# A 3x3 filter of one of three channel blocks on TensorE as 32x32 diagonal tiles, in place of VectorE

## The chip, the cores and the metric

One core of a Trainium2 chip runs the whole program. The metric is device microseconds of one execution, lower is better. TensorE (PE; PEld for its weight loads), VectorE (DVE), ScalarE (ACT) and GpSimd (POOL) work side by side, each in the order of its own queue; the queue of SyncE (SP) issues the transfers. Matrix products land in PSUM banks, from which VectorE or ScalarE copy them out ("evacuate") to SBUF.

## The reference, cut to what matters

32 images of 56 x 56 tokens and 96 channels, fp32, pass through four layers. The change is in layer 0.

```python
# layer 0: x is [32, 56, 56, 96]; E = 4 experts, M = 384 hidden channels
rw = sigmoid(mean(x, (1, 2)) @ Wr + br)                  # router: [32, 4]
h = einsum('bhwc,bcm->bhwm', x, einsum('be,ecm->bcm', rw, Wpw)) + rw @ bpw
h = relu(bn1(h))                                         # 384 channels
h = sum_e rw[:, e] * (conv3x3_depthwise(h, Wdw[e]) + bdw[e])   # <- the filter in question
h = relu(bn2(h))
h = einsum('bhwm,bmf->bhwf', h, einsum('be,emf->bmf', rw, Wpwl)) + rw @ bpwl
x = bn3(h) + x
# layer 1: x + a fixed 5x5 depthwise filter
# layer 2: relu, 3x3 depthwise filter, 96x96 pointwise product, batch norm
# layer 3: windows of 7x7 of the image shifted by 3: layer norm, attention of 3 heads with
#          a mask, projection, residual; layer norm, gelu perceptron 96-384-96, residual
```

A depthwise filter treats each channel by itself. Since the experts are mixed linearly, one mixed kernel of nine taps per channel and image is enough.

## The kernel before, in words

Channels lie on partitions for layers 0 to 2, tokens for layer 3. The 384 hidden channels are three blocks of 128 (`NB`). The image is worked in two halves of 28 rows for layer 0, in 8-row strips for layer 1 (`conv5`, L368) and in rows of windows, 7 image rows or 392 tokens, for layers 2 and 3.

`stage_conditional` is layer 0 of one image. It loads and transposes the image (L216, L231, L232), finds the router weights (L242 to L251; one small product on L246), and mixes the experts: `wmix` and `wmix2`, the weights of the two pointwise products, and `mix`, per channel the nine taps and two biases. `biasd` and `s2` are the bias and scale of the second batch norm. Then, for each half and block k:

- `expand` multiplies by `wmix` in four pieces (L293) and ScalarE evacuates them with batch norm and relu into `h1` (L300), a block with a border of zeros that GpSimd sets (L286 to L289). There are two `h1` buffers, and a block is expanded ahead of the filter of the block before it.
- The filter is nine VectorE instructions over 128 x 1568 elements: L324 multiplies the first tap's view by its tap, L326 multiplies the next view and adds.
- ScalarE applies batch norm and relu to the block (L329).

When the three blocks of a half stand in `h2` (one buffer), four products per half sum over the blocks (L344), ScalarE evacuates them (L352), and GpSimd adds the image into `x1` (L353), which layer 1 reads.

`stage_depthwise` is layers 1 and 2: 25 diagonal 96x96 products a strip on TensorE (L368, evacuated on L377), a 3x3 filter of 96 channels on VectorE (L390, L392), a GpSimd copy of the border (L393), and a product (L402, L409). `stage_swin` is layer 3: `normalized` and `transposed` for the norms (L448 to L466, with L83 and L84 for the reciprocal root), projections (L478 to L490), scores per head (L502 to L515, on 32 rows of TensorE), weighted sums per head (L527 to L535, on 32 columns of it), L543, and the perceptron (L559, L560, L566, L574, stores on L581 to L588).

Three images are under way, each in another stage. The stages are Python generators, and `interleave` draws their steps side by side, each at an even pace by its number of steps (91, 44 and 42), which sets the order on every engine:

```python
stages.append((stage_conditional(step), 42))
interleave(stages)
```

All products but those of the attention share the four PSUM banks of the pool `mm`; `att` has three and one more for `po`. A strip of layer 1 holds its bank from its first to its 25th product, across many steps of the others.

Of the kernel before, what the change touches and what calls it, by code (L numbers as in the profile page):

```python
# [11 lines left out]
F32 = mybir.dt.float32  # L12
AF = mybir.ActivationFunctionType
# [5 lines left out]
C = 96  # L19
M = 384  # L20
E = 4
P = 128
NB = 3  # blocks of 128 among the 384 hidden channels
NROW = 8  # rows of windows, 7 image rows each
RT = 7 * W  # tokens of a row of windows
PK = 98  # tokens of a pack: two neighbouring windows, a block of 7 x 14 tokens
NP = 4  # packs in a row of windows
NH = 3
# [5 lines left out]

# columns of the 384-channel vectors
V_BPW, V_BDW, V_G1, V_B1, V_M1, V_V1, V_G2, V_B2, V_M2, V_V2, V_MLP, V_WDW = 0, 4, 8, 9, 10, 11, 12, 13, 14, 15, 16, 17
NV = V_WDW + 36
# columns of the 96-channel vectors
U_BPWL, U_G3, U_B3, U_M3, U_V3, U_DWB, U_LN1G, U_LN1B, U_LN2G, U_LN2B, U_DWK = 0, 4, 5, 6, 7, 8, 9, 10, 11, 12, 13
# [3 lines left out]
def attention_mask():  # L43
    """Additive mask of a pack's 98 x 98 scores: [ordinary or last row of windows, query, pack, key]."""
    m = np.zeros((2, PK, NP, PK), np.float32)
    r, c = np.divmod(np.arange(PK), 14)
    for last in range(2):
        for j in range(NP):
            col = 14 * j + c
            group = col // 7 * 10  # L50
            group = group + np.where(col >= 53, 1, 0)
            if last:
                group = group + np.where(r >= 4, 5, 0)
            m[last, :, j, :] = np.where(group[:, None] == group[None, :], 0.0, NEG)
    return m
# [3 lines left out]
def kernel(ctx: ExitStack, tc: tile.TileContext, a: dict, mask: bass.AP, out: bass.AP):  # L59
# [11 lines left out]

# [1 line left out]
    ident = const.tile([P, P], F32, name="ident")  # L73
# [6 lines left out]
    def rsqrt(dst, src, eps, scale=1.0):  # L80
        """dst = 1 / sqrt(src * scale + eps), for few elements."""
        n = src.shape[0]
        nc.vector.tensor_scalar(dst, src, scale, eps, ALU.mult, ALU.add)  # L83
        nc.gpsimd.tensor_tensor(dst, dst, mhalf[:n, : dst.shape[1]], ALU.pow)  # L84
# [50 lines left out]

    # batch norms of layer 0 as scale * y + shift
    def bn(g, b, m, v, n, name):
# [11 lines left out]

    # what the router mixes per channel: nine taps and two biases, experts innermost  # L150
    NM = 11
# [6 lines left out]

    # layer 1: its kernel's taps on diagonals, the residual in the centre's
    k5 = load([C, 25], a["L1_conv_kernel"].rearrange("c a b -> c (a b)"), "k5")  # L160
# [4 lines left out]

    # layer 2: pointwise weights scaled by its batch norm, and the biases in one row
    pw = load([C, C], a["L2_conv_pw_kernel"].rearrange("a b c f -> (a b c) f"), "pw")
# [19 lines left out]

    # layer 3
    wq = load([C, C], a["L3_conv_wq"], "wq")
# [8 lines left out]

    # images with zero borders
    x1 = big.tile([C, H + 4, W + 4], F32, name="x1")  # L200
# [3 lines left out]

    # rows of x1 that layer 1 of the image before no longer reads
    consumed = [H]

    def stage_conditional(b):
        """Layer 0 of image b, into x1."""
        xT = two.tile([C, H * W], F32, tag="xT", name="xT")  # L210
# [28 lines left out]

        # router, the same on all partitions  # L240
        pooled = small.tile([C, 1], F32, tag="pooled", name="pooled")
# [10 lines left out]

        # mixtures of the experts
        wmix = work.tile([C, M], F32, tag="wmix", name="wmix", bufs=1)
# [18 lines left out]
        nc.vector.tensor_tensor(biasd, mix[:, :, 10], s2, ALU.mult)  # L273
        nc.vector.tensor_tensor(biasd, biasd, t2, ALU.add)
        prod3 = small.tile([C, E], F32, tag="prod3", name="prod3", bufs=2)
        nc.vector.tensor_tensor(prod3, c96[:, U_BPWL : U_BPWL + E], rw[:C], ALU.mult)
# [5 lines left out]
        def expand(half, k):  # L282
            # rows first .. first + 28 of the image at rows at .. of h1; the row beyond the image is zero
            first, at = (0, 1) if half == 0 else (HALF - 1, 0)
            h1 = two.tile([P, HALF + 2, W + 2], F32, tag="h1", name="h1")
            nc.gpsimd.memset(h1[:, :, 0:1], 0.0)  # L286
            nc.gpsimd.memset(h1[:, :, W + 1 : W + 2], 0.0)
            edge = 0 if half == 0 else HALF + 1
            nc.gpsimd.memset(h1[:, edge, :], 0.0)  # L289
            r = 0  # L290
            for n in (8, 7, 7, 7):
                pt = mm.tile([P, 512], F32, tag="mm", name="pt")
                nc.tensor.matmul(  # L293
                    pt[:, : n * W],
                    wmix[:, k * P : (k + 1) * P],
                    xT[:, (first + r) * W : (first + r + n) * W],
                    start=True,
                    stop=True,
                )
                nc.scalar.activation(  # L300
                    h1[:, at + r : at + r + n, 1 : W + 1],
                    pt[:, : n * W].rearrange("p (r w) -> p r w", w=W),
                    AF.Relu,
                    bias=bias1[:, k : k + 1],
                    scale=s1[:, k : k + 1],
                )
                r += n
            return h1

        # a block's expansion is traced ahead of the filter of the block before  # L310
        blocks = [(half, k) for half in range(2) for k in range(NB)]
        h1 = expand(*blocks[0])
        yield
        for at, (half, k) in enumerate(blocks):
# [3 lines left out]
            acc = h2[:, k].rearrange("p (r w) -> p r w", w=W)  # L318
            for t in range(9):
                dy, dx = divmod(t, 3)  # L320
                tap = mix[:, k, t : t + 1]
                view = h1[:, dy : dy + HALF, dx : dx + W]
                if t == 0:
                    nc.vector.tensor_scalar(acc, view, tap, None, ALU.mult)  # L324
                else:
                    nc.vector.scalar_tensor_tensor(acc, view, tap, acc, ALU.mult, ALU.add)  # L326
                if t % 3 == 2:
                    yield
            nc.scalar.activation(  # L329
                h2[:, k], h2[:, k], AF.Relu, bias=biasd[:, k : k + 1], scale=s2[:, k : k + 1]  # L330
            )
            h1 = h1_next
# [4 lines left out]
            for n in range(4):  # L337
                r = half * HALF + 7 * n
                # the image before has to have left these rows of x1
                while consumed[0] < r + 7:  # L340
                    yield
                pt = mm.tile([P, 512], F32, tag="mm", name="pt")
                for q in range(NB):
                    nc.tensor.matmul(  # L344
                        pt[:C, :RT],
                        wmix2[:, q * C : (q + 1) * C],
                        h2[:, q, n * RT : (n + 1) * RT],
# [13 lines left out]
    def stage_depthwise(b, res):  # L361
        """Layers 1 and 2, from x1 to res: tokens of the shifted image on partitions."""
        def conv5(i):
# [51 lines left out]

        # a row's matrix product is traced well behind its filter
        packed = []
        done = 0
        for i in range(7):
            for n, _ in enumerate(conv5(i)):  # L420
                yield
                if n == 1 and packed:
                    pointwise()
                    # rows up to 8 i - 2 have both neighbours
                    if 7 * done + 10 < 8 * i:
# [19 lines left out]
    def normalized(src):  # L445
        """src, [98, 4, 96] with tokens on partitions, less its mean and by its deviation."""
        mu = small.tile([PK, NP], F32, tag="mu", name="mu")
# [12 lines left out]
    def transposed(d, g, bta):  # L460
        """The layer norm of a normalized d, with channels on partitions."""
        pt = mm.tile([P, 512], F32, tag="mm", name="pt")
# [6 lines left out]
    def stage_swin(b, res):  # L469
        """Layer 3 on the shifted image in res, packs of two windows on partitions."""  # L470
        def project(i):
# [78 lines left out]
        def perceptron(i):  # L550
# [25 lines left out]
            )  # L576
            # back to the unshifted image; the last rows and columns wrap around
            for j in range(NP):
# [11 lines left out]

        # a row's weighted sums are traced behind the scores of the next row
        rows_of, probs, normed = {}, {}, {}
# [24 lines left out]
    def interleave(stages):  # L617
        """Traces the stages' steps side by side, each at an even pace by its number of steps."""
        todo = [[0, n, g] for g, n in stages]
# [5 lines left out]

    # three images at a time, each in another part of the chain
    residuals = {}
    for step in range(B + 2):
# [7 lines left out]
        if step < B:  # L636
            stages.append((stage_conditional(step), 42))
        interleave(stages)


def build(nc, shapes, batch):
    """The program on nc for inputs of these shapes."""
    a = {k: nc.dram_tensor(f"in_{k}", s, F32, kind="ExternalInput").ap() for k, s in shapes.items()}
# [17 lines left out]
```

## Time and profile before

| | |
|---|---|
| median of 2 runs | 10090.53 us (10088.93 to 10092.14) |
| span of the profiled execution | 10095.2 us |
| mean granted TensorE clock | 0.974 |
| TensorE busy | 9488.0 us, 94%, 47622 matmuls |
| VectorE busy | 7154.6 us, 71% |
| ScalarE busy | 4210.8 us, 42% |
| GpSimd busy | 3729.8 us, 37% |
| DMA | mean 9 GB/s |

The first row is from unprofiled runs; everything below it is one profiled execution. Busy time is the union of an engine's instructions, and matmuls are pipelined: the recorded length of one contains time in which the next already streams, so the spacing of their starts says more than their length. "idle before, releaser" tells how long an engine stood still before a group's instructions and what ended most of that.

In the profile, the program is a ramp of two periods (first only layer 0, then layers 0 to 2), 30 alike with all three stages, and a tail in which the last images leave.

### The profile page before, as it was taken

To read this page: it belongs to the slowest core of one execution; us is meant where nothing else is said; L and a number is where in the kernel's file an instruction comes from. 1 tells how busy PE (TensorE), PEld (TensorE's weight loads), DVE (VectorE), ACT (ScalarE), POOL (GpSimd) and SP (SyncE) were. 2 spreads that over 40 slices of the span, in tenths; PEclk is the share of its full clock that TensorE was granted. 3 is DMA by queue.
4 is the path that set the end of the run, shared out by engine and by line. 5 is a ranking of instruction groups with operands and counts; after the bars stand their busy time and mean duration, and the time that the engine had idled before them with its cause. 6 is when DMAs were issued, how large, how long until landed. Compare 5 with 4: busy or idle time off the path is not lost.

```text
span 10095.2 us, 132019 instructions
## 1 busy us (share of the span) xinstructions
PE 9488.0 (94%) x47622; PEld 5516.7 (55%) x47622; DVE 7154.6 (71%) x11221; ACT 4210.8 (42%) x11520; POOL 3729.8 (37%) x3406
## 2 busy tenths in 40 slices
PE   5999999999999999999999999999999999999998
PEld 2455555555555555555555555555555555555556
DVE  6767767678777677676787776776767877767743
ACT  2344444444444444444444444444444444444434
POOL 2234334334333343333433333433434433334323
PEclk8999999999999999999999999999999999999996
DMA  0000000000000000000000000000000000000000
GB/s 21 5 10 7 6 9 11 10 9 6 7 10 10 10 7 6 9 10 10 9 6 7 10 10 10 7 6 9 10 10 9 6 7 10 10 10 7 4 5 9
DMA packets 164927, 88.06 MB, mean 9 GB/s; under 512 B 138455, under 2 KB 164272, under 8 KB 164272
## 3 DMA queue, kind: packets, MB, share of 16 engines
q1 hardware_dynamic: 164272, 79.62, 3.0%
q8 instruction: 375, 6.14, 0.2%
q14 instruction: 280, 2.29, 0.1%
HBM read 40.95 MB, written 38.54 MB: 8 GB/s over the span
## 4 chain that ended last, share of the span: by engine, by line
PE 77%; DVE 10%; POOL 6%; ACT 3%; issue 2%; SPq 1%; DMA 0%; POOLq 0%; DVEq 0%; ACTq 0%
PE pt L368 37%; PE po L535 6%; PE pt L566 5%; PE ps L502 5%; PE pt L344 4%; PE pt L293 4%; DVE d L392 4%; PE pt L559 3%; DVE h L326 3%; POOL lnd L457 2%; PE ps L527 2%; PE pt L478 2%; PE pt L543 2%; POOL var L84 2%; PE pt L482 2%
## 5 line engine op out<-in xcount | busy, mean ns | idle before, releaser
L368 PE MATMUL pt<-x,diag 96*96 96x448 f32 x11200 | 4643.9, 549 | 9.9 <-ACT h L300 9.9
L326 DVE SCALAR_TENSOR_TENSOR h<-h,mix,h 128x1568 f32<-128x1568 f32 x1536 | 2887.5, 1888 | 4.3
L368 PEld LDWEIGHTS pt<-x,diag 96*96 96x96 f32 x11200 | 1683.3, 163 | 1765.3 <-issue 1670.8
L515 POOL TENSOR_TENSOR s<-s,den 98x392 f32<-98x392 f32 x768 | 822.5, 1071 | 2480.1 <-DVE den L514 2469.5
L392 DVE SCALAR_TENSOR_TENSOR d<-x,c,d 96x392 f32<-96x392 f32 (+2 forms) x2304 | 1470.0, 649 | 11.2 <-ACT x L377 7.6
L511 ACT ACTIVATE s<-s,top 98x98 f32<-98x98 f32 x3072 | 1114.6, 366 | 475.7 <-DVE top L508 475.1
L84 POOL TENSOR_TENSOR var<-var,mhalf 98x4 f32<-98x4 f32 x512 | 714.3, 1395 | 784.3 <-DVE var L83 536.2
L504 DVE TENSOR_TENSOR s<-ps,masks 98x392 f32<-98x392 f32 x768 | 429.0, 559 | 647.4 <-PE ps L502 646.7
L552 POOL TENSOR_TENSOR tb<-res,L_conv_b 98x384 f32<-98x384 f32 x256 | 506.3, 1978 | 1029.9 <-DVE res L546 567.8
L566 PE MATMUL pt<-w,hid 128*98 128x96 f32 x6144 | 693.1, 266 | 171.4 <-ACT hid L560 159.4
L566 PEld LDWEIGHTS pt<-w,hid 128*98 128x98 f32 x6144 | 657.5, 179 | 322.6 <-ACT hid L560 242.6
L535 PEld LDWEIGHTS po<-pT,v 98*32 98x32 f32 x6144 | 508.2, 111 | 508.0 <-ACT pT L532 334.0
L502 PEld LDWEIGHTS ps<-kT,qT 32*98 32x98 f32 x6144 | 589.0, 164 | 324.6 <-issue 248.5
L492 POOL TENSOR_TENSOR xb<-res,L_conv_bo 98x384 f32<-98x384 f32 x256 | 451.1, 1762 | 836.4 <-DVE res L546 592.2
L457 POOL TENSOR_TENSOR lnd<-lnd,var 98x384 f32<-98x384 f32 x512 | 724.9, 1416 | 40.2
L535 PE MATMUL po<-pT,v 98*32 98x98 f32 x6144 | 678.3, 254 | 64.5 <-ACT pT L532 49.1
L502 PE MATMUL ps<-kT,qT 32*98 32x98 f32 x6144 | 713.9, 258 | 3.3 <-ACT qT L479 3.3
L300 ACT ACTIVATE h<-pt,bias,s 128x392 f32<-128x392 f32 (+1 forms) x768 | 497.6, 687 | 381.9 <-PE pt L293 342.3
L559 PE MATMUL pt<-hT,w 96*128 96x392 f32 x1536 | 562.0, 502 | 86.3 <-ACT hT L466 86.2
L466 ACT ACTIVATE hT<-pt,c 96x392 f32<-96x392 f32 x512 | 342.7, 669 | 705.2 <-PE pt L464 705.1
L344 PE MATMUL pt<-h,wmix 128*96 128x392 f32 x1536 | 568.8, 501 | 61.2 <-ACT h L329 37.7
L293 PE MATMUL pt<-xT,wmix 96*128 96x392 f32 (+1 forms) x1536 | 583.8, 514 | 28.6 <-ACT h L300 24.5
(112 smaller groups left out, 10735.7 us busy)
## 6 DMA issues: line engine op xcount, KB each, us to landing
xin<-in_x SPq DMA_DIRECT2D x256, 147.0 KB
out<-o SPq DMA_DIRECT2D x1792, 4.1 KB
out<-o SPq DMA_DIRECT2D x1792, 1.1 KB
out<-o SPq DMA_DIRECT2D x672, 36.8 KB
out<-o SPq DMA_DIRECT2D x96, 21.0 KB
out<-o SPq DMA_DIRECT2D x96, 15.8 KB
wpw<-in_L_conv_Wpw SPq DMA_DIRECT2D x1, 576.0 KB
wpwl<-in_L_conv_Wpwl SPq DMA_DIRECT2D x4, 144.0 KB
```

The source lines that it names most:

```text
L84: nc.gpsimd.tensor_tensor(dst, dst, mhalf[:n, : dst.shape[1]], ALU.pow)
L293: nc.tensor.matmul(pt[:, : n * W], wmix[:, k * P : (k + 1) * P], xT[:, (first + r) * W : (first + r + n) * W], start=True, stop=True,)
L326: nc.vector.scalar_tensor_tensor(acc, view, tap, acc, ALU.mult, ALU.add)
L344: nc.tensor.matmul(pt[:C, :RT], wmix2[:, q * C : (q + 1) * C], h2[:, q, n * RT : (n + 1) * RT], start=(q == 0), stop=(q == NB - 1),)
L368: nc.tensor.matmul(o, diag5[:, t], x1[:, 8 * i + dy : 8 * i + dy + 8, dx : dx + W], start=(t == 0), stop=(t == 24),)
L392: nc.vector.scalar_tensor_tensor(acc, view, tap, acc, ALU.mult, ALU.add)
L457: nc.gpsimd.tensor_tensor(d, d, var[:, :, None].to_broadcast([PK, NP, C]), ALU.mult)
L502: nc.tensor.matmul(ps[:PK, js], qT[hs, js], kT[hs, js], start=True, stop=True)
L511: nc.scalar.activation(s[:, j], s[:, j], AF.Exp, bias=top[:, j : j + 1], accum_out=den[:, j : j + 1])
L535: nc.tensor.matmul(po[hs, js], v[:, j, hs], pT[:, js], start=True, stop=True)
L559: nc.tensor.matmul(pt[:, :RT], w1[:, k * P : (k + 1) * P], hT, start=True, stop=True)
L566: nc.tensor.matmul(pt[:PK, j * C : (j + 1) * C], hidden[k][:, j * PK : (j + 1) * PK], w2[:, k], start=(k == 0), stop=(k == NB - 1),)
```

## The change

The third block of each half (k = 2) is filtered on TensorE. A tap of a block is a diagonal 128x128 matrix; only its four 32x32 diagonal tiles are not zero, and these are multiplied by themselves, each on its own 32 rows and 32 columns of the array. Two row chunks of 392 tokens are done at a time, in two banks: the first writes tile g to output partitions of group g, the second ("turned") to those of the next group, so that the eight products of a tap use eight different tiles of the array. The turned chunk thus comes out with its channels rotated by 32 partitions, and the bias, the scale and the weights of the next product are kept in a rotated copy as well (`biasdt`, `s2t`, `wmix2t`), made by two small transfers each in the SyncE queue. `taps` holds the nine diagonals of an image.

```diff
+    eye32 = const.tile([P, 32], F32, name="eye32")
+    nc.vector.tensor_tensor(eye32, ident[:, 0:32], ident[:, 32:64], ALU.add)
+    nc.vector.tensor_tensor(eye32, eye32, ident[:, 64:96], ALU.add)
+    nc.vector.tensor_tensor(eye32, eye32, ident[:, 96:128], ALU.add)
+
+    def turn(dst, src):
+        nc.sync.dma_start(out=dst[32:], in_=src[:96])
+        nc.sync.dma_start(out=dst[:32], in_=src[96:])
+
+    s2t = const.tile([P, 1], F32, name="s2t")
+    turn(s2t, s2[:, NB - 1 :])
...
+        wmix2t = work.tile([P, C], F32, tag="wmix2t", name="wmix2t", bufs=1)
+        turn(wmix2t, wmix2[:, (NB - 1) * C :])
+        biasdt = small.tile([P, 1], F32, tag="biasdt", name="biasdt", bufs=2)
+        turn(biasdt, biasd[:, NB - 1 :])
+        taps = work.tile([P, 9, 32], F32, tag="taps", name="taps")
+        nc.vector.tensor_tensor(
+            taps,
+            eye32[:, None, :].to_broadcast([P, 9, 32]),
+            mix[:, NB - 1, 0:9, None].to_broadcast([P, 9, 32]),
+            ALU.mult,
+        )
...
-            for t in range(9):
+            if k == NB - 1:
+                for pair in range(2):
+                    banks = [mm.tile([P, 512], F32, tag="mm", name="pt") for _ in range(2)]
+                    for t in range(9):
+                        dy, dx = divmod(t, 3)
+                        for turned in range(2):
+                            r = 7 * (2 * pair + turned) + dy
+                            for g in range(4):
+                                to = 32 * ((g + turned) % 4)
+                                nc.tensor.matmul(
+                                    banks[turned][to : to + 32, :RT].rearrange("c (r w) -> c r w", w=W),
+                                    taps[32 * g : 32 * g + 32, t],
+                                    h1[32 * g : 32 * g + 32, r : r + 7, dx : dx + W],
+                                    start=(t == 0),
+                                    stop=(t == 8),
+                                )
+                    for turned in range(2):
+                        at = (2 * pair + turned) * RT
+                        nc.scalar.activation(
+                            h2[:, k, at : at + RT],
+                            banks[turned][:, :RT],
+                            AF.Relu,
+                            bias=biasdt if turned else biasd[:, k : k + 1],
+                            scale=s2t if turned else s2[:, k : k + 1],
+                        )
+                    yield
+            for t in range(9) if k < NB - 1 else ():
...
-            nc.scalar.activation(
-                h2[:, k], h2[:, k], AF.Relu, bias=biasd[:, k : k + 1], scale=s2[:, k : k + 1]
-            )
+            if k < NB - 1:
+                nc.scalar.activation(
+                    h2[:, k], h2[:, k], AF.Relu, bias=biasd[:, k : k + 1], scale=s2[:, k : k + 1]
+                )
...
-                        wmix2[:, q * C : (q + 1) * C],
+                        wmix2t if n % 2 and q == NB - 1 else wmix2[:, q * C : (q + 1) * C],
...
-            stages.append((stage_conditional(step), 42))
+            stages.append((stage_conditional(step), 40))
```

## The prediction

> **What bounds the kernel now.** I read the page first: engines, chain, costliest groups.
>
> ```profile
> PE 9488.0 (94%) x47622; PEld 5516.7 (55%) x47622; DVE 7154.6 (71%) x11221; ACT 4210.8 (42%) x11520; POOL 3729.8 (37%) x3406
> PE 77%; DVE 10%; POOL 6%; ACT 3%; issue 2%; SPq 1%; DMA 0%; POOLq 0%; DVEq 0%; ACTq 0%
> L368 PE MATMUL pt<-x,diag 96*96 96x448 f32 x11200 | 4643.9, 549 | 9.9 <-ACT h L300 9.9
> L326 DVE SCALAR_TENSOR_TENSOR h<-h,mix,h 128x1568 f32<-128x1568 f32 x1536 | 2887.5, 1888 | 4.3
> ```
>
> TensorE is busy 94% of the span and carries 77% of the chain that ended last; VectorE, where the filter sits (L326), has 29% of the span free. Counts matter too: L368 is called 32 x 7 x 25 = 5600 times and appears 11200 times, so an fp32 matmul is two passes here, each with a weight load.
>
> Next the windows view over the 28 periods from 746 to 9380 us, in which three images are under way (a period, from one router matmul on L246 to the next, is 308.3 us), and the waits of TensorE in the same stretch:
>
> ```profile
> 746.00:9380.00 8634.00, 8230.00 (x41662) 4777.92 (x41662) 6259.54 (x9772) 3678.55 (x10080) 3274.12 (x2968) 0.99 0.03 9
> PE pt L566 <- ACT hid L560: 147.9, 57, 4.0
> PE pt L464 <- POOL lnd L457: 91.5, 56, 1.7
> PE pt L559 <- ACT hT L466: 77.4, 84, 1.1
> PE po L535 <- ACT pT L532: 46.5, 85, 1.9
> PE pt L478 <- ACT h L300: 15.1, 28, 0.6
> PE po L535 <- DVE pT L530: 11.2, 29, 0.4
> PE pt L566 <- DVE res L409: 11.0, 28, 0.4
> ```
>
> The columns are length, then busy time of PE, weight loads, DVE, ACT and POOL, then the granted clock. TensorE idles (8634 - 8230) / 28 = 14.4 us a period, at clock 0.99, and nearly all of it is ended by ScalarE or GpSimd, not by the filter. VectorE is busy 224 of 308 us. Work taken off VectorE can therefore give back a part of 14.4 us a period; work put on TensorE is paid almost in full.
>
> Last, the timeline, for what passes cost and whether small ones overlap (start, length, count at the end):
>
> ```profile
> 5013.13 0.82 PE L482 MATMUL pt<-hT,wk 96*96 96x392 f32 x2
> 5011.53 0.93 PE L502 MATMUL ps<-kT,qT 32*98 32x98 f32 x8
> 5005.64 1.36 PE L502 MATMUL ps<-kT,qT 32*98 32x98 f32 x16
> 5036.32 0.86 PE L535 MATMUL po<-pT,v 98*32 98x98 f32 x8 [0.20 <-ACT pT L532]
> 9806.91 1.24 PE L535 MATMUL po<-pT,v 98*32 98x98 f32 x16
> ```
>
> Of two 392-column passes (L482) the second adds 0.33 us; start to start of such passes is 329 ns at the median (L344, L293, L559 alike). L502 uses 32 rows of the array per head, L535 32 columns per head. Eight passes of one head follow at 84 to 87 ns. Sixteen of two heads would need 1.6 us in a row, and take 1.36 and 1.24: in the single starts, the second head's first pass begins 4 to 5 ns after the first head's fifth, and then both go on at 82 to 89 ns each. So passes on different rows, and passes on different columns, do run side by side at full pace, two at a time. More than two is not shown.
>
> **The change, part by part.** *Removed*, a third of the block filter: from VectorE 2887.5 / 3 + 219.6 / 3 (L324) = 1036 us, 32 us a period; from ScalarE a third of L329, 108 us. *Added to ScalarE*: 256 evacuations of 128x392, at L300's 676 ns = 173 us. Net +65 us, 2 us a period, on an engine 42% busy: hidden; were it the bound, +65 us. *Added to VectorE*: the 128x288 product `taps`, nearest the 128x288 step of L259 at 0.51 us, 16 us in all, hidden in the 84 us that VectorE has free a period. *Added to SyncE*: four small copies an image for `wmix2t` and `biasdt` (behind them in the queue stand stores of finished rows, which come only in the last third of a swin stage), and two for `s2t`, ahead of the loads of the later constants and of the first image. There the queue waits for s2, written at 14.96 us where SyncE stood at 13.66; two issues at about 0.4 us: +2 us at the start, once.
>
> *Added to TensorE*, which decides: 32 images x 2 halves x 2 pairs x 9 taps x 2 x 4 = 9216 calls, 18432 passes of 392 columns. L502 and L535, the small ones of before, are two passes as well. One after the other they cost 329 ns: 6064 us. The eight tiles of a tap differ in rows, columns or both. Ends for a pass: 41 ns with eight at once (758 us), 165 ns with the two at once that the trace shows (3032 us). I take 46 ns: in the L535 pair the second head's first pass starts 370 ns after the first head's, so TensorE took in eight passes with their weight loads in that time, and no row shows it faster: 848 us. The two kinds of pair shown are the two relations that neighbours among the eight have, and no pair slowed its partner.
>
> [...] Here four row tiles write one bank, on different partitions; the L502 pair wrote two banks, so no run here shows it. [...]
>
> Ends of a burst: 128 bursts of 144 passes. Changing between L368 and the column-tiled L535 costs 91 ns more than staying (466 against 375 ns into it, 175 against 84 out of it); twice that and 0.16 us until the eight are under way are 0.35 us: 44 us. TensorE gains 892 us of work, 27.9 us in each of 32 periods.
>
> *Waits.* In the period of 5064 to 5373 us one stretch of the chain runs through the block filter, while the layer-2 filter and a GpSimd copy stand behind it:
>
> ```profile
> 5102.88 1.80 DVE h L326
> 5108.78 0.96 DVE d L392
> 5109.73 1.76 DVE h L326
> 5112.10 2.31 POOL d L393
> ```
>
> It costs TensorE 0.71 + 1.38 us around it. With a third of the filter gone, and the bursts giving ScalarE and GpSimd time to catch up, I take 4 us a period back; bounds 0 and 14.4. Against it, each burst needs two of the four `mm` banks while a layer-1 sum holds one and the next block's expansion fills the rest, so up to three L300 evacuations (2 us) may stand before it, with every later matmul behind it: 0 to 8 us a period, taken as 3. The stage's pace, 40 steps in place of 42, moves work by less than one step: nothing.
>
> *The ramp.* In the first period TensorE is idle anyway, but the next half's filter waits for `h2` and so for L344. A half's third block took 8 x 1.86 + 1.03 us of VectorE and 1.70 of ScalarE; two bursts take 13.9 us and an evacuation: -3 us a half, -6. In the second period TensorE streams only some 150 of 238 us: nothing, with -10 and +28 as bounds.
>
> Sum: 30 x (27.9 - 4 + 3) = 807, -6, +2: +803 us on the profiled 10095.2 us, 10898. The median of the runs, 10090.5, lies 4.7 us below that span: **10893 us**, 8% slower. Its own range: 10406 (41 ns, all idle time recovered, no new waits) to 11163 (46 ns, nothing recovered, 8 us of new waits).
>
> **Rivals.** *Four at once.* Tiles on the same rows take turns, 82 ns a pass: 1511 + 44 us, 48.6 a period; 30 x 47.6 + 16 in the first period + 2 = +1446: 11536 us. For it: the L502 pair is on different rows. Against: the L535 pair shares all its rows and overlapped.
> *Two at once*, or banks that exclude one another: 3032 + 44, 96.1 a period, +2884 and some 110 in the first two periods: 13085 us. For it: no row has more than two. Against: in neither pair did the second stream slow the first. *One at a time* gives 190.9 a period and about 16100 us; both pairs speak against it.
> *Not slower.* The place is VectorE's in-order queue: if the filter's 1.9 us instructions are what holds up the softmax and norm chains that TensorE waits for, their removal pays for the bursts. Beyond plain streaming, the starts of matmuls show 39.5 us a period, idle time, mode changes and short waits together. To end within 2% (202 us, 6.7 a period) 21.2 of these must vanish at 46 ns, 18.4 at 41 ns; at 25 recovered the time is about 10175. For it: L326 is the next largest group after L368. Against: idle time is 14.4 of the 39.5, ended by ScalarE and GpSimd.
>
> **How the numbers follow.** Eight tiles mostly side by side 0.64, four at once 0.16, two at once 0.07, one at a time 0.03, not slower 0.07, the rest between these. Range 10600 to 11600: the first case but for its lower tail, and the second. About 2% is what a measurement of this kernel can tell from no change. Faster by over 2% needs 34.6 of the 39.5 us to vanish: 0.02; within 2%: 0.05; slower: 0.93.
>
> **What would show it.** Right: about 66000 matmul records; the new line at 18432 passes, bursts of 6 to 7 us, a period near 335 us; VectorE's busy time down by about 1020 us; TensorE busy 95% or more. Bursts of 12 us mean four at once, of 24 two. Wrong altogether: a period at or below 308 us, or new waits ahead of the bursts above 8 us a period.

## The result and the profile after

The changed kernel takes 10602.98 us (10600.68 to 10605.28), the kernel before 10090.53 us: a ratio of 1.050, 95% interval 1.048 to 1.052. It is slower, as forecast, by 512 us where 802 were forecast, at the lowest end of the range. The profiled execution spans 10598.9 us at a granted clock of 0.983.

From the page of the changed kernel, engines, chain and the groups that answer to those of before (layer 1 is now L420, the block filter on VectorE L377, the new passes L353):

```profile
PE 10242.0 (97%) x66054; PEld 5897.7 (56%) x66054; DVE 6153.5 (58%) x10680; ACT 4283.1 (40%) x11712; POOL 3451.2 (33%) x3406
PE 86%; DVE 9%; ACT 2%; issue 1%; POOL 1%; SPq 0%; DMA 0%; DVEq 0%; ACTq 0%; POOLq 0%
L420 PE MATMUL pt<-x,diag 96*96 96x448 f32 x11200 | 4582.1, 545 | 0.0
L377 DVE SCALAR_TENSOR_TENSOR h<-h,mix,h 128x1568 f32<-128x1568 f32 x1024 | 1916.0, 1878 | 3.5
L353 PE MATMUL pt<-h,taps 32*32 32x392 f32 x18432 | 850.2, 504 | 97.2 <-ACT h L362 74.2
```

VectorE is 1001 us lighter, and L353 has 18432 passes. Their 504 ns are the length of one, which overlaps others: together they keep TensorE busy for 850 us, 46 ns each with the ends of the bursts and passes at half clock among them. TensorE carries 86% of the chain in place of 77%; GpSimd has nearly left it, 1% after 6%.

The timeline shows the four bursts of one period, the fourth in two rows (start, length, count):

```profile
5064.14 6.31 PE L353 MATMUL pt<-h,taps 32*32 32x392 f32 x144
5075.08 6.16 PE L353 MATMUL pt<-h,taps 32*32 32x392 f32 x144
5193.95 6.16 PE L353 MATMUL pt<-h,taps 32*32 32x392 f32 x144
5200.51 0.86 PE L353 MATMUL pt<-h,taps 32*32 32x392 f32 x8
5203.84 7.83 PE L353 MATMUL pt<-h,taps 32*32 32x392 f32 x136 [2.47 <-ACT h L362]
```

A burst without a wait takes 5.67 to 5.82 us from its first to its last start, some 40 ns a pass (40.4 below). The single starts show passes mostly 6 to 8 ns apart, all eight in a row or, in the first burst of a period, four and, 180 ns behind the first of them, the four of the other chunk; each tile follows again after 329 ns: eight streams at full pace. The fourth burst follows 0.4 us behind the third; after eight passes it waits for the third's banks, which ScalarE is still to evacuate (L362). That makes it 8.98 us long; in 17 of 28 periods it takes 10.67 us, because after the wait TensorE also runs 3.4 us at half clock.

The windows view over 27 periods, 1084 to 9868 us (length, busy time of PE, weight loads, DVE, ACT and POOL, then the clock), and TensorE's waits in them:

```profile
1084.00:9868.00 8784.00, 8576.66 (x55734) 4928.44 (x55732) 5188.19 (x8966) 3610.19 (x9882) 2934.81 (x2862) 0.99 0.03 9
```

```profile
PE pt L618 <- ACT hid L612: 70.6, 28, 2.6
PE pt L353 <- ACT h L362: 66.8, 27, 2.5
PE pt L611 <- ACT hT L518: 59.7, 81, 1.1
PE po L587 <- ACT pT L584: 5.6, 27, 0.2
```

TensorE idles (8784 - 8577) / 27 = 7.7 us a period, 14.4 before. The wait for the norm on GpSimd (`lnd`, 91.5 us before) is gone, that for `pT` nearly so, that for `hid` halved; the one for the banks is new.

One accounting serves all runs below. From the starts of TensorE's passes, each gap is compared with the spacing of such passes back to back (375 ns for 448 columns, 329 for 392, 83 for 98); over 100 ns beyond it counts as a wait, 40 to 100 as a mode change ("changes and less" adds what is under 40), and time from start to start inside bursts is counted apart. In us a period:

| | period | streaming | changes and less | waits | bursts |
|---|---|---|---|---|---|
| before | 308.4 | 269.5 | 19.5 | 19.4 | |
| after | 325.4 | 270.8 | 19.8 | 7.6 | 27.2 |

So the bursts cost 27.2 + 1.3 (their last passes) + 0.3, and 11.8 of waits went away: +17.0 a period, 510 us in 30 periods.

A wait of this accounting is not only standing still: TensorE is idle in 14.4 of the 19.4 us and in 5.2 of the 7.6, and recorded busy in the rest, with the end of the pass ahead or with a slower pass. In the same periods the clock stood at half for 8.2 us a period before and 4.6 after; 1.7 of the 5.0 us of recorded work and 0.1 of the 2.4 lie in gaps that touch such a stretch.

### The profile page after: what moved, and what is told of

It reads as the page before. It is cut to its first block, busy times and chain, and to the rows that moved or that the text cites. A ratio compares the mean times of both kernels' runs of the same rounds, so it can differ in the third digit from the quotient of the medians.

```text
span 10598.9 us, 168961 instructions
## 1 busy us (share of the span) xinstructions
PE 10242.0 (97%) x66054; PEld 5897.7 (56%) x66054; DVE 6153.5 (58%) x10680; ACT 4283.1 (40%) x11712; POOL 3451.2 (33%) x3406
## 4 chain that ended last, share of the span: by engine, by line
PE 86%; DVE 9%; ACT 2%; issue 1%; POOL 1%; SPq 0%; DMA 0%; DVEq 0%; ACTq 0%; POOLq 0%
PE pt L420 37%; PE ps L554 6%; PE pt L353 6%; PE po L587 6%; PE pt L396 5%; PE pt L618 5%; PE pt L318 4%; DVE h L377 4%; DVE d L444 4%; PE pt L611 4%; PE ps L579 2%; PE pt L530 2%; PE pt L539 2%; PE pt L595 2%; PE pt L534 2%; PE pt L454 2%
## 5 line engine op out<-in xcount | busy, mean ns | idle before, releaser
L420 PE MATMUL pt<-x,diag 96*96 96x448 f32 x11200 | 4582.1, 545 | 0.0
L420 PEld LDWEIGHTS pt<-x,diag 96*96 96x96 f32 x11200 | 1678.6, 162 | 1760.0 <-issue 1683.9
L377 DVE SCALAR_TENSOR_TENSOR h<-h,mix,h 128x1568 f32<-128x1568 f32 x1024 | 1916.0, 1878 | 3.5
L444 DVE SCALAR_TENSOR_TENSOR d<-x,c,d 96x392 f32<-96x392 f32 (+2 forms) x2304 | 1408.1, 630 | 294.8 <-ACT x L429 277.1
L84 POOL TENSOR_TENSOR var<-var,mhalf 98x4 f32<-98x4 f32 x512 | 674.9, 1318 | 1124.1 <-DVE var L83 1094.3
L353 PE MATMUL pt<-h,taps 32*32 32x392 f32 x18432 | 850.2, 504 | 97.2 <-ACT h L362 74.2
L604 POOL TENSOR_TENSOR tb<-res,L_conv_b 98x384 f32<-98x384 f32 x256 | 469.2, 1833 | 1058.7 <-DVE res L598 800.3
L618 PE MATMUL pt<-w,hid 128*98 128x96 f32 x6144 | 667.4, 260 | 81.2 <-ACT hid L612 79.4
L353 PEld LDWEIGHTS pt<-h,taps 32*32 32x32 f32 x18432 | 401.6, 107 | 503.6 <-issue 357.3
L544 POOL TENSOR_TENSOR xb<-res,L_conv_bo 98x384 f32<-98x384 f32 x256 | 330.1, 1289 | 993.6 <-DVE res L598 784.6
L509 POOL TENSOR_TENSOR lnd<-lnd,var 98x384 f32<-98x384 f32 x512 | 618.7, 1208 | 40.1
```

The source lines that it names most:

```text
L353: nc.tensor.matmul(banks[turned][to : to + 32, :RT].rearrange("c (r w) -> c r w", w=W), taps[32 * g : 32 * g + 32, t], h1[32 * g : 32 * g ...
L420: nc.tensor.matmul(o, diag5[:, t], x1[:, 8 * i + dy : 8 * i + dy + 8, dx : dx + W], start=(t == 0), stop=(t == 24),)
L509: nc.gpsimd.tensor_tensor(d, d, var[:, :, None].to_broadcast([PK, NP, C]), ALU.mult)
L618: nc.tensor.matmul(pt[:PK, j * C : (j + 1) * C], hidden[k][:, j * PK : (j + 1) * PK], w2[:, k], start=(k == 0), stop=(k == NB - 1),)
```

## The experiments

Unless an interval is given, a run is one execution with a profile, beside a run of the kernel before (10087 to 10111 us). Theory A: the waits left because VectorE's queue got shorter. Theory B: because the others catch up during a burst. Theory D, formed on the way: because the three stages meet in another order.

**Load VectorE again.**

```diff
+                    spare = big.tile([P, 24, W], mybir.dt.bfloat16, tag="spare", name="spare")
+                    for t in range(5) if pair == 0 else range(4, 9):
...
+                        nc.vector.scalar_tensor_tensor(spare, view, tap, centre, ALU.mult, ALU.add)
                     yield
```

> The changed kernel, with VectorE loaded again: beside the bursts it does ten instructions over 24 rows of the third block (into a spare tile that nothing reads), about the work that was taken off it. Theory A (relief): the 11.8 us a period by which TensorE's waits shrank, 19.4 to 7.6, came from VectorE's shorter queue; loaded again, they return, 30 x 11.8 = 354 us: about 10955. Theory B (cover): the waits shrank because other engines catch up while TensorE works through a burst; then the load costs little: 10600 to 10650.

10931.5 us: 328 us more, as A says (the load comes in lumps of five instructions, where the filter's came in threes). Only 3.9 us a period are returned as plain waits (11.5); 6.0 stand inside the bursts (33.2), where the banks come free later. From 784 to 9800 us of this run, where the changed kernel had 66.8 in its stretch:

```profile
PE pt L353 <- ACT h L362: 155.3, 27, 5.9
```

**Relief without bursts.** The third block is not filtered at all; L329 reads `h1`.

> The kernel before without the third block's filter on any engine: ScalarE's batch norm and relu read the expanded block instead, so the output is not the reference's; all else and the pace of 42 steps stay. Theory A (relief): 11.8 us a period fall away, and 2 x 16 us in the first period: about 10090 - 354 - 40 = 9700. Theory B (cover): only the ramp gains: about 10050.

9973.9 us: 114 us below the run of before beside it, far from A's 390; some 36 of them fall in the first two periods. The waits fall from 19.4 to 15.1, that is 4.2 us a period, and 1.4 return as mode changes. So the relief by itself is worth what the prediction took, and A does not explain 11.8; nor does the result of the first run fit B. Each theory failed once.

**Same tiles for both chunks.**

```diff
-                                to = 32 * ((g + turned) % 4)
+                                to = 32 * g
```

> The changed kernel with both chunks of a pair on the same four diagonal tiles (second chunk not turned; rotated copies are made but not used). If the two chunks overlap only because they use different tiles, a pass costs 82 ns in place of 41, a burst 11.8 us in place of 5.9, 23.6 us a period: about 10603 + 700 = 11300, less what the longer bursts cover (up to 7 us a period, 11090). If what sets the pace of a burst is how fast TensorE takes in instructions, nothing changes: about 10600.

11227.6 us. From this run's timeline:

```profile
5177.35 12.06 PE L353 MATMUL pt<-h,taps 32*32 32x392 f32 x144
```

81 ns a pass from start to start: chunks on the same tile took turns, chunks on neighbouring tiles of the same rows did not (40.4 ns in the changed kernel). Turning the second chunk is worth 19 us a period. The waits stay at 7.7: bursts of twice the length cover no more of them.

**Every burst twice.**

```diff
-                    for t in range(9):
+                    for t in [*range(9), *range(9)]:
```

> The changed kernel with every burst's nine taps done twice (the second time starts the sums anew, so the output is the same). It adds 576 passes of 40.4 ns, 23.3 us a period. If TensorE now bounds the period with nothing left to win, it is paid in full: 30 x 23.3 + 20 in the ramp = +720, about 11320. Theory B (cover) lets the longer bursts cover more of the 7.6 us of waits that are left: +17 a period, about 11110.

11263.0 us, bursts 46.9 us a period, waits 7.8. The second nine taps cost 23.3 less the 3.9 us of the bank wait, which is gone, now that there is time to evacuate. TensorE's added work is paid in full, and B falls in the form that longer bursts cover more.

**One step between the bursts of a half.**

```diff
                     yield
+                    if pair == 0:
+                        yield
-            stages.append((stage_conditional(step), 40))
+            stages.append((stage_conditional(step), 42))
```

> The changed kernel with one more step of the other stages between the two bursts of a half (42 steps in place of 40). In the changed kernel the fourth burst of a period stands 0.4 us behind the third, starts eight passes and waits for the third's banks to be evacuated: bursts take 27.2 us a period where four of 5.8 would take 23.3. If that wait comes from the two bursts standing together, it goes: 30 x 3.9 = -117, about 10485. If the evacuations are late whatever stands between (ScalarE's queue), or the shift brings other waits, the time stays at 10600.

11017.0 us. The bank wait is gone as meant (bursts 23.2), but the waits elsewhere rise from 7.6 to 23.5 us a period; the clock stands at half for 23.3 us a period (4.6 in the changed kernel), and in 10.5 of the 23.5 TensorE is recorded busy. One step more in one stage undid more than all that the change had won: from here comes theory D.

**Bursts of one tap.** The filter of the third block is left out but for its centre.

> The changed kernel with bursts of one tap (the centre) in place of nine, so that the filter of the third block is left out but for its centre and the output is not the reference's. TensorE has 20.7 us less to do a period. The relief of VectorE alone left 15.1 us of waits (run e2), the changed kernel has 7.6, and bursts of double length 7.8. Theory B2 (cover by the length of the bursts): with hardly any burst the waits go back to about 15: period 325.4 - 3.9 - 20.7 + 7.5 = 308, total about 10080. Theory D (order): the waits left because the work of the stages meets in another order, so they stay at 7.6 to 8: period 301, total about 9860.

9915.0 us. With bursts of 2.1 us a period in all, the waits are 10.2, nearer D's 8 than B's 15.

**One number.** `interleave` draws a step from the stage that is furthest behind its number of steps. Changing that number for layer 0 adds and removes no instruction.

```diff
-            stages.append((stage_conditional(step), 42))
+            stages.append((stage_conditional(step), 40))
```

> The changed kernel with one number back as it was: layer 0 is paced as if it had 42 steps, and still has 40. No instruction is added or removed. Theory A/B (relief of VectorE and cover by the bursts made the waits of TensorE shrink from 19.4 to 7.6 us a period): 10600, within 50. Theory D (the pace sets the order in which the three stages meet, and with it the waits; one step more, run e5, already brought 23.5 us of waits): the waits change by several us a period, the time by 100 us or more, most likely up, to 10700 to 11000.

> The kernel before with the pace number of the changed one: layer 0 paced as if it had 40 steps. Nothing else changes. Theory A/B: as before, 10090 within 50. Theory D: the waits move between 8 and 24 us a period, the time by 100 us or more either way; if 40 is the lucky number in itself, 11 us a period fall away: about 9750.

> The kernel before with layer 0 paced as if it had 44 steps. As for 40: no change by theory A/B, 100 us or more either way by theory D. The two runs together give the spread that the order alone makes in a kernel without any bursts.

> The kernel before, layer 0 paced as if it had 41 steps. Theory D alone (the order sets the waits, bursts or not): among a few pace numbers some give waits as low as the changed kernel's 7.6 us a period, a time down to 9750. Theory D2 (the low waits need the bursts too, which give the other engines time): without bursts the waits stay at 15 us or more at any pace, 9950 or more.

> The kernel before, paced as if layer 0 had 43 steps. As for 41: theory D a time anywhere from 9750 to 10480; theory D2 9950 or more.

> The changed kernel, paced as if layer 0 had 38 steps. Theory D: waits anywhere from 7 to 25 us a period as in the kernel before, 10550 to 11050. Theory D2: waits below those of the kernel before at most paces, 7 to 17 us, 10550 to 10800.

> The changed kernel, paced as if layer 0 had 44 steps: as for 38.

> The kernel before at pace 46. Of five paces (40 to 44) the waits of TensorE were 29.6, 24.1, 19.4, 11.5 and 19.0 us a period. If a faster pace of layer 0 is better in itself, they are below 15 here: under 9970. If the order is a lottery, anything from 9850 to 10480, about 10130 the mean of the five.

| pace number | before: us, waits a period | after: us, waits a period, bursts |
|---|---|---|
| 38 | | 10621.9, 11.1, 23.4 |
| 40 | 10478.5, 29.6 | **10603.0**, 7.6, 27.2 |
| 41 | 10269.6, 24.1 | |
| 42 | **10090.5**, 19.4 | 10774.5, 17.1, 22.8 |
| 43 | 9855.6, 11.5 | |
| 44 | 10161.8, 19.0 | 10531.7, 9.3, 22.9 |
| 46 | 10604.6, 34.5 | |

The pace alone moves the kernel before between 9856 and 10605 us, more than the change did, and the changed kernel by 243. The granted clock is the lower the longer the time: 0.942, 0.956, 0.974, 0.978, 0.957 and 0.935 at 40, 41, 42, 43, 44 and 46 of the kernel before, and at 46 TensorE is recorded busy in half of the 34.5 us (17.8). Whether it is the waits that bring the clock down was not tried. At 40, with TensorE's waits from 1084 to 9368 us, it is the norm chain that the kernel before waits for most:

```profile
PE pt L464 <- POOL lnd L457: 184.1, 52, 4.3
PE pt L293 <- ACT hid L560: 85.0, 52, 2.2
PE pt L402 <- ACT dp L395: 81.6, 26, 3.1
```

Theory D holds, but not alone, and not within its stated bounds: pace 44 moved the kernel before by 53 us, where 100 or more were expected, 40 brought 29.6 us of waits, where 24 were the most named, 46 a time above its 10480, and the changed kernel at 44 ended just below its 10550. D2, without bursts 9950 or more at any pace, falls with 43. The mean of the waits is 23.0 us over six paces of the kernel before and 11.3 over four of the changed one, in which they are lower at each of the three numbers that both ran. At a like number the change costs 125, 684 and 370 us (40, 42, 44). Paired instead by the distance from its own count of steps (before 40, 42, 44, 46 with after 38, 40, 42, 44), it costs 143, 512 and 613 us and gains 73; best against best, 9856 and 10532, it costs 676. The 11.8 us do not split into two fixed parts either: by way of the changed kernel at 42 the change takes 2.3 and the number 9.5; by way of the kernel before at 40 the number adds 10.2 and the change takes 22.0. So part of the 11.8 us goes with the change (4.2 by relief alone), and the rest depends on the order; how much is cover by the bursts is not settled by so few paces.

**The kernel before at pace 43, timed.**

> The kernel before with layer 0 paced as if it had 43 steps, once more and timed: 9855 us, 2.4% below the kernel before, within 0.3%. If the first look was a chance of one run and not of the order, it falls back towards 10100.

9844.0 us (9828.5 to 9857.9), ratio to the kernel before 0.974, interval 0.972 to 0.977. It beats both, by a number. TensorE's waits from 738 to 9300 us:

```profile
PE pt L559 <- ACT hT L466: 95.0, 57, 2.8
PE pt L566 <- ACT hid L560: 54.9, 57, 2.8
PE pt L464 <- POOL lnd L457: 12.4, 29, 0.5
```

The same instructions run, 47622 passes on TensorE; the wait for `lnd` shrinks from 91.5 to 12.4 us.

**Tiles where TensorE already works.** If tiles overlap so well, layer 1, 96 channels of diagonals, should gain.

```diff
+            halves = [mm.tile([P, 512], F32, tag="mm", name="pt") for _ in range(2)]
...
+                            halves[n][32 * (g + n) : 32 * (g + n) + 32, : 4 * W].rearrange("c (r w) -> c r w", w=W),
+                            diag5[gs, t, gs],
+                            x1[gs, r : r + 4, dx : dx + W],
```

> The kernel before, its block filter on VectorE as it was, with layer 1 (L368, the costliest group) on 32x32 diagonal tiles: a strip of 8 rows is two halves of 4 rows, the second half one column group to the right in a bank of its own, so that six passes of 224 columns run side by side; the second half comes out 32 partitions further and is evacuated in three pieces. If six overlap as the eight did, a strip takes 50 x 187 ns = 9.4 us in place of 19, 68 us a period less on TensorE: period about 255 (VectorE's 224 us busy come near), total about 8550. If taking in passes at 31 ns is too fast and 41 ns is the limit: 86 us in place of 65 for layer 1, total about 9100. If the rows' tiles exclude each other here: no gain, 10100 or more.

> v1 with the tiles only in strips 1, 3 and 5 of layer 1; the other four strips keep the 96x96 form. In v1 the granted clock was 0.83: the trace has stretches of 82 us at half clock in which TensorE stood still for under 2 us and ran layer 1's tiles and the small products of the attention. If full-array work is what brings the clock back, it is over 0.95 here, TensorE has 28 us a period less to do, and with some more waits the period is about 290: 9550. If the clock stays at 0.83 with these few tiles too, nothing is won: 10300 or more.

> The changed kernel with layer 1 on tiles as in v1. If TensorE still bounds the period, it is slower than v1 by the price of the bursts, up to 25 us a period (+750). If VectorE bounds it by then, taking 32 us a period off it pays at last, and this is faster than v1: about 8300. Between the two lies about 8500.

10424.3, 10423.1 and 11352.7 us, with clocks of 0.83, 0.89 and 0.80. The first has the time of its last case, but not its reason; the second came out as "nothing is won", with a clock above v1's and short of the 0.95; the third misses by far. The six streams do overlap, six passes in 191 ns at full clock, 32 ns each. But the clock falls to 0.50 and stays there for 82 us at a time. The windows view of v1 (length, busy time of PE, weight loads, DVE, ACT, POOL, then the clock):

```profile
1936.80:2056.20 119.40, 113.16 (x1446) 73.69 (x1444) 72.51 (x148) 62.34 (x193) 40.36 (x42) 1.00 0.06 16
2056.20:2138.00 81.80, 80.89 (x708) 47.22 (x714) 50.09 (x63) 23.76 (x75) 29.84 (x20) 0.50 0.01 1
```

For 82 us TensorE is busy all but 0.9 us, at half clock. In the kernel before no such stretch between 758 and 9300 us is longer than 6.8 us. Why it stays down no run shows. TensorE stood still for 25.8 us a period in v1, 14.4 before, and a wait of 4.41 us ends at 1733.22 us, just after another such stretch begins (1732 to 1813.9 us, clock 0.50); but within the 82 us shown it hardly stood still. Nor were small tiles alone enough to hold the clock at half, as far as eight at a time go: in the 17 long fourth bursts of the changed kernel it was back at full after 3.4 us with nothing but 32x32 passes in between.

## Why the prediction was right or wrong

- *TensorE bounds, and added work is paid.* Right: 18432 passes, TensorE at 97%, and doubled bursts were paid in full. The period is 325.4 us, forecast near 335.
- *The price of a pass* was 46 ns, measured 40.4: the rate at which passes are taken in, drawn from the start of the second head, was no limit (they start 6 to 8 ns apart); what came is eight streams at full pace, 329 / 8 = 41. 3.2 us a period too much. That the page's busy time comes to 46 ns too is chance: it holds the ends of the bursts. The two kinds of pair in the trace of before did carry over to eight.
- *The waits taken away* were the step that failed most: 4 us a period, with 14.4 as the bound, and 11.8 came, 234 us over 30 periods. The 4 were meant for relief and for catching up during the bursts; relief without bursts gave 4.2, of which 1.4 came back as mode changes. What the step left out is the order: the change takes two steps out of layer 0 and lowers the pace number with them. "The stage's pace, 40 steps in place of 42, moves work by less than one step: nothing" is the sentence that the runs refute: that number alone moved the kernel before by 388 us, and the changed kernel, left at 42, has waits of 17.1 us in place of 7.6 and takes 171 us more. How the 11.8 divide between relief, cover and order stays open.
- *New waits for banks* were taken as 3 us a period, 3.9 came, all in the fourth burst after its first eight passes, behind L362 and not the L300 that was named; about 1 of it is passes at half clock behind that wait.
- *The ends of a burst*, 1.4 us, came as 1.6. These four terms, 7.8 + 3.2 - 0.9 - 0.2, are the 9.9 us a period between forecast and measurement.
- *The ramp*: the start came 1.7 us later (2 forecast), the first period fell by 3.6 us (6 forecast), the second by 3.6 too (nothing forecast).
- *Four at once, two at once, one at a time*: refuted by 40.4 ns, where 82, 165 and 329 were forecast. Nor did banks exclude one another here: four row tiles wrote one bank, on different partitions, mostly 6 to 7 ns apart.
- *Not slower* would have needed 21.2 us of waits to vanish a period. Of the 39.5 us (38.9 by the accounting above), 11.8 vanished.

## What to carry to other kernels

A kernel whose stages are interleaved by hand has a hidden parameter in every step count: before a change is credited or blamed, run the kernels before and after at a few neighbouring paces, and see what the order alone does. Work moved onto the engine that bounds was paid nearly in full here, however well it overlapped with itself (the second nine taps: 23.3 us a period, less a bank wait of 3.9); relief of an engine that does not bound gave back 3 to 4 us of the 32 taken off it (its period fell by 2.9). And a cheaper form of the same work was no gain where the granted clock fell with it (layer 1 on tiles: 0.83 in place of 0.974, 10424.3 us in place of 10101.3): look at the granted clock of a variant first.

## What the runs showed of the hardware that was not expected

Eight 32x32 tiles in two banks ran fully side by side in fp32, some 40 ns a pass where a stream alone takes 329, and six of 224 columns at 32 ns a pass. Two chunks on the same tile took turns, 81 ns. With layer 1 on tiles the clock stayed at 0.50 for 82 us, in which TensorE was busy for 80.9; busy time alone did not bring it back there.
